# Row transposes of the rotation taken from the pair sums through DRAM, with the pair sums' additions moved behind their transposes

## The chip, the cores and the metric

One core of a Trainium2 chip runs the whole program in float32. The metric is the device time of one execution in microseconds (us). Ratios are computed as the mean time of one kernel's fast runs over the mean of the other's fast runs of the same rounds, so a ratio is not quite the quotient of the medians that stand beside it.

The engines: PE is the matrix engine, DVE the vector engine, ACT the scalar engine, Pool is GpSimd, and SP is SyncE, which here only issues DMAs. "SPq" in a profile is the queue of SP's instructions.

## The reference, cut to what matters

x is 8 images of 256 channels and 96 x 96 pixels. Two residual layers follow each other, each behind a group norm:

```python
x = x + fft_attention(gn(x))       # q, k, v = fft2(1x1 convolutions); per-head 32x32 attention of
                                   # normalized spectra; |ifft2|; 1x1 convolution
x = x + linear_attention(gn(x))    # q, k = softplus(convolutions to 32 channels)
```

The kernel never makes a spectrum. It uses that the attention needs covariances of x with itself and with x mirrored in both directions. With e = x + mirrored x and o = x - mirrored x, these are the sums of e e^T and o o^T over pixels: the **pair sums**. The value path is a multiplication of every image row by a matrix of circulant windows, called R below: the **rotation**.

## The kernel before

A batch (an image) goes through these stages: attention matrices, rotation, images (the |ifft2| and its projection), linear attention, output. The pair sums of the next batch are woven into the last three as filler for PE; what is left of them behind the output is called the tail. Batch 0's sums have nothing to be woven into and stand alone at the start.

In the pair sums, DVE or Pool add whole image rows first; PE then transposes e and o, ACT evacuates them (copies them out of PSUM, where PE has written them: 598 ns for 128x512, the median), and PE multiplies:

```python
def even_odd(b, u):                      # rows PR*u.. and their mirror (cut)
    for c in range(2):
        op = (eng.tensor_add, eng.tensor_sub)[c]
        op(d[:, :, lo:hi, 1:W], x_t[:, :, ra:ra + n, 1:W], x_t[:, :, back, W - 1:0:-1])
        ...
# pair_sums, per chunk of 128 columns:
        for c in range(2):
            for k in range(KC):
                nc.tensor.transpose(pt[...], eo[:, c, k, i:i + np_], ident)
        nc.scalar.activation(t[0:np_, :, 0:C], pt[...], AF.Copy, scale=weight)
        if pending is not None:
            products(*pending, first, False)      # acc += t^T t for e and o
```

The rotation, two rows at a time, transposes the rows again (xr), lets ACT evacuate them, and multiplies two steps later (y):

```python
nc.tensor.transpose(pt[0:W, ...], x_of(b)[:, k, o:o + W], ident)                      # xr
nc.tensor.matmul(pu[:, o:o + W + 1], lhsT=gt[0:W, r, ...], rhs=tm[:, g % TR + r, :])  # y
```

`tm` is a window of R, read from DRAM by ACT's queue in runs of 384 bytes.

## Time and profile before

| | before |
|---|---|
| time, median of 3 runs | 2765.28 us (2764.82 to 2765.53) |
| span of the profiled run | 2760.7 us |
| start to the end of batch 0's sums | 75.7 us |
| a batch (1 to 6): rotation / images / linear attention / output and what is between / tail | 73.0 / 142.0 / 69.0 / 41.1 / 14.2 to 15.3 us |

The stage times are differences between the first starts of PE's instructions that open each stage: the group norm's matmul, the images' first matmul, the second group norm, the denominators, the first output product.

The slices (each digit is a fortieth of the span, in tenths; 9 is 90% or more):

```profile
PE   8999999999999999999999999999999999999988
PEclk9999999999999999999999999999999999999997
```

PE is busy in every slice (8 or 9 tenths), and its granted clock is at 9 (90% or more) in every slice but the last, which has 7. The waits of PE (line, what it waited for, us in total, times, longest):

```profile
PE eoT L350 <- POOL eo L318: 10.4, 15, 7.3
PE kT L770 <- DVE arena L748: 3.6, 1, 3.6
PE acc L331 <- ACT xT L353: 3.5, 7, 0.5
```

All waits of PE together, 2760.7 - 2719.5 = 41 us, are smaller than 2% of the span. The table of stretches for batch 0's sums (stretch, length, busy PE, weight loads, DVE, ACT, Pool, clock, DMA share, GB/s):

```profile
0.00:20.00 20.00, 12.51 (x71) 11.29 (x72) 13.98 (x41) 5.43 (x9) 16.00 (x77) 1.00 0.94 320
20.00:60.00 40.00, 40.00 (x278) 37.50 (x277) 35.61 (x76) 13.46 (x23) 20.48 (x27) 1.00 0.37 112
60.00:75.70 15.70, 15.70 (x110) 14.75 (x109) 0.00 (x0) 5.36 (x10) 0.00 (x0) 1.00 0.16 51
```

From 20 us on PE has no gap. In the first 20 us the loads of x fill the DMA engines (share 0.94).

### The profile page before, as it was taken

How to read it: one execution, taken by the hardware profiler on the slowest of the kernel's cores; microseconds unless marked ns; L12 is line 12 of the kernel's file. 1: busy time of each engine (PE TensorE's matmuls, PEld its weight loads, DVE VectorE, ACT ScalarE, POOL GpSimd, SP SyncE). 2: the span in 40 equal slices, each digit the busy share in tenths (PEclk: the TensorE clock that was granted, in tenths of full speed). 3: DMA queues.
4: the chain of work that ended last, by engine and by line, in shares of the span. 5: the costliest groups of instructions: out<-in, count | busy, mean ns of one | idle time of the engine just before them, and what ended most of it. 6: DMA issues, size and time to landing. Idle time of an engine off the chain costs nothing.

```text
span 2760.7 us, 47785 instructions
## 1 busy us (share of the span) xinstructions
PE 2719.5 (99%) x18348; PEld 1972.5 (71%) x18348; DVE 1958.4 (71%) x4104; ACT 1366.5 (49%) x2098; POOL 841.5 (30%) x939
## 2 busy tenths in 40 slices
PE   8999999999999999999999999999999999999988
PEld 8965679657795677956679566885678856788556
DVE  7588666876668767587675875769766687676776
ACT  3455634556345563355634546345453455544553
POOL 5033340342403423035230351313513135131311
PEclk9999999999999999999999999999999999999997
DMA  5120151201512015120151201521015210251003
GB/s 169 40 65 11 47 184 43 67 9 49 179 43 73 6 47 182 43 69 6 54 179 46 63 6 54 182 54 52 7 53 184 58 46 7 62 178 28 0 7 138
DMA packets 197274, 192.50 MB, mean 70 GB/s; under 512 B 88821, under 2 KB 197049, under 8 KB 197049
## 3 DMA queue, kind: packets, MB, share of 16 engines
q1 hardware_dynamic: 129800, 164.34, 18.8%
q10 hardware_dynamic: 67248, 25.12, 3.6%
q8 instruction: 146, 2.39, 0.4%
q14 instruction: 80, 0.65, 0.1%
HBM read 113.85 MB, written 75.57 MB: 69 GB/s over the span
## 4 chain that ended last, share of the span: by engine, by line
PE 94%; DVE 3%; ACT 2%; DMA 1%; issue 1%; POOL 0%; SPq 0%; POOLq 0%; DVEq 0%; ACTq 0%
PE z L621 21%; PE po L633 18%; PE acc L331 13%; PE y L553 10%; PE xr L550 6%; PE eoT L350 5%; PE xT L779 5%; PE kq L718 5%; PE o L863 4%; PE kx L755 3%; DMA arena<-in_x_dram 1%; PE cw L423 1%; PE kT L770 1%; DVE arena L559 1%; PE mz L511 1%
## 5 line engine op out<-in xcount | busy, mean ns | idle before, releaser
L621 PE MATMUL z<-arena,mz 128*128 128x384 f32 (+2 forms) x2400 | 595.0, 476 | 0.0
L633 PE MATMUL po<-e,wo 128*128 128x384 f32 x1536 | 529.7, 486 | 0.2 <-ACT e L668 0.2
L667 POOL TENSOR_TENSOR e<-e 128x768 f32<-128x768 f32 x192 | 348.2, 1815 | 554.1 <-ACT e L666 554.1
L621 PEld LDWEIGHTS z<-arena,mz 128*128 128x128 f32 (+1 forms) x2400 | 325.6, 163 | 241.4 <-issue 42.4
L553 PE MATMUL y<-tm,xT 96*128 96x97 f32 x3040 | 472.6, 261 | 1.7 <-ACT sd_a L288 0.5
L553 PEld LDWEIGHTS y<-tm,xT 96*128 96x128 f32 x3040 | 457.8, 192 | 12.5 <-issue 4.9
L331 PE MATMUL acc<-xT 128*128 128x256 f32 (+2 forms) x2368 | 440.5, 328 | 3.5 <-ACT xT L353 3.5
L633 PEld LDWEIGHTS po<-e,wo 128*128 128x128 f32 x1536 | 289.4, 190 | 197.7 <-DVE arena L635 1.2
L662 DVE TENSOR_TENSOR e<-z,xT 128x768 f32<-128x768 f32 x384 | 365.7, 953 | 85.2 <-PE z L621 85.2
L264 DVE BATCH_NORM_STATS2 st<-arena 128x6 f32<-128x384 f32 x768 | 406.5, 552 | 13.7 <-DMA arena<-in_x_dram 3.2
L550 PE MATMUL xr<-ident,arena 128*96 128x128 f32 x1520 | 409.2, 275 | 0.0
L331 PEld LDWEIGHTS acc<-xT 128*128 128x128 f32 (+1 forms) x2368 | 380.2, 191 | 37.7 <-ACT xT L353 5.2
L563 ACT COPY xT<-xr 96x512 f32<-96x512 f32 (+1 forms) x384 | 220.2, 578 | 293.8 <-PE xr L550 289.4
L666 ACT ACTIVATE e<-e 128x1536 f32<-128x1536 f32 x192 | 284.6, 1482 | 93.5 <-DVE e L662 92.3
L668 ACT ACTIVATE e<-e 128x768 f32<-128x768 f32 x192 | 161.9, 843 | 334.0 <-POOL e L667 332.9
L317 POOL TENSOR_TENSOR eo<-arena 128x760 f32<-128x760 f32 x136 | 246.1, 1809 | 253.7 <-issue 130.1
L635 DVE TENSOR_TENSOR arena<-arena,po 128x384 f32<-128x384 f32 x384 | 211.1, 551 | 92.6 <-PE po L633 69.5
L353 ACT ACTIVATE xT<-eoT 128x512 f32<-128x512 f32 x280 | 166.6, 598 | 183.9 <-PE eoT L350 182.2
L550 PEld LDWEIGHTS xr<-ident,arena 128*96 128x96 f32 x1520 | 227.2, 150 | 10.3 <-issue 6.9
L559 DVE COPY arena<-y 128x384 f32<-128x384 f32 (+1 forms) x384 | 209.7, 547 | 1.2 <-issue 0.5
L558 DVE COPY ys<-y 128x4 f32<-128x4 f32 (+1 forms) x384 | 62.4, 162 | 199.3 <-PE y L553 195.9
L350 PE MATMUL eoT<-ident,eo 128*128 128x128 f32 (+1 forms) x1184 | 188.1, 280 | 10.4 <-POOL eo L318 10.4
(202 smaller groups left out, 2907.0 us busy)
## 6 DMA issues: line engine op xcount, KB each, us to landing
arena<-in_x_dram SPq DMA_DIRECT2D x184, 384.0 KB
out_dram<-arena SPq DMA_DIRECT2D x184, 384.0 KB
tm<-rt ACTq DMA_DIRECT2D x112, 216.0 KB
tm<-rt SPq DMA_DIRECT2D x16, 216.0 KB
arena<-in_x_dram SPq DMA_DIRECT2D x8, 288.0 KB
out_dram<-arena SPq DMA_DIRECT2D x8, 288.0 KB
wl<-in_w1t_dram SPq DMA_DIRECT2D x8, 256.0 KB
wl<-in_w2t_dram SPq DMA_DIRECT2D x8, 256.0 KB
```

Of the source, the lines that this page charges most:

```text
L264: nc.vector.bn_stats(out=st[:, k, c, :], in_=x_of(b)[:, k, c * CH:(c + 1) * CH])
L317: op(d[:, :, lo:hi, 1:W], x_t[:, :, ra:ra + n, 1:W], x_t[:, :, back, W - 1:0:-1])
L331: mm = nc.tensor.matmul(acc[c][:, m * C:m * C + (KC - m) * P], lhsT=t[0:np_, c, m * P:(m + 1) * P], rhs=t[0:np_, c, m * P:C], start=(first ...
L350: nc.tensor.transpose(pt[0:np_, c * C + k * P:c * C + (k + 1) * P], eo[:, c, k, i:i + np_], ident)
L550: nc.tensor.transpose(pt[0:W, r * C + k * P:r * C + (k + 1) * P], x_of(b)[:, k, o:o + W], ident)
L553: nc.tensor.matmul(pu[:, o:o + W + 1], lhsT=gt[0:W, r, k * P:(k + 1) * P], rhs=tm[:, g % TR + r, :], start=True, stop=True)
L559: nc.vector.tensor_copy(y[:, :, :, g + r:g + 2], src[:, :, W - 1::-1, r:2])
L621: mm = nc.tensor.matmul(out[:, o:o + n * W], lhsT=columns(mz, k, c, j), rhs=y[:, k, h * W:(h + n) * W], start=(k == 0 and o == 0), stop=(k ...
L633: nc.tensor.matmul(po[:, 0:CH], lhsT=wo[:, k, m * P:(m + 1) * P], rhs=e[:, k, :], start=(k == 0), stop=(k == KC - 1))
L662: nc.vector.tensor_add(e[:, 2 * c:2 * c + 2, :].rearrange("p t (q h) -> p t q h", h=H), pz[:, 0:CH].rearrange("p (q h) -> p q h", h=H).uns ...
L666: nc.scalar.activation(e, e, AF.Square)
L667: nc.gpsimd.tensor_add(e[:, 0:2, :], e[:, 0:2, :], e[:, 2:4, :])
```

## The change

The intent: PE transposes x itself in the pair sums, not e and o; the additions come behind the evacuation, on Pool. The transposes of six tiles of twelve are then at hand as plain transposed rows. SP writes them to DRAM (`xtd`), and the rotation reads them from there, so that PE need not transpose these rows a second time; such rows are called **spilled**. R is written once to DRAM in pieces laid out as they are used (`rx`). The diff, cut to its core:

```diff
+T0 = 6
-    for t in range(NT - 1, -1, -1):
+    for t in range(NT - 1, NT - 5, -1):
         load_x(0, t)                          # the rest is loaded tile by tile within batch 0's sums
+    rx = dram.tile([H // TR, W, TR, W + 1], F32, name="rx")
+    xtd = dram.tile([2, (H // 2 - PR * T0) * W, C], F32, name="xtd")
 ... pair_sums, per chunk j (0 to 2) of tile t:
+            if not b and j == 0 and t >= 4:
+                load_x(0, t - 4)
+            for k in range(KC):
+                nc.tensor.transpose(pt[:, 0, k * P:(k + 1) * P], front[:, k], ident)
+                nc.tensor.transpose(pt[:, 1, k * P:(k + 1) * P], back[:, i % 2, k], ident)
+            nc.scalar.activation(both, pt, AF.Copy, scale=pw[:, j:j + 1])
+            if t >= T0:
+                n = P - j // 2
+                for c in range(2):
+                    nc.sync.dma_start(out=turned(c, PR * t, 1 + P * j)[0:n], in_=both[0:n, c])
+            eo = sum_slot()[:, :, 0:C]
+            if b or j % 2:
+                nc.gpsimd.tensor_add(eo[:, 0], both[:, 0], both[:, 1])
+                nc.gpsimd.tensor_sub(eo[:, 1], both[:, 0], both[:, 1])
+            else:                             # batch 0, even chunks: DVE, straight from PSUM
+                ...
 ... rotation:
+        def spilled(h):
+            return PR * T0 <= h < H - PR * T0 and h != H // 2
+        def fetch(i):                         # three steps ahead
+            nc.sync.dma_start(out=xts[i][0:W, :, 0:C], in_=rows.rearrange("(r w) n -> w r n", w=W))
+            step(None if spilled(h) else h, ...)   # no transposes where the rows come from DRAM
```

Cut: the tables, the copies that bring the mirrored side into order (`back`; by Pool, and by ACT for tiles 0 to 5 of batches 1 to 7), the order of the pieces of R, and small changes in how often chunks are woven in.

A tile has 384 columns in three chunks of 128, shifted by one column, so that the last chunk holds one column that is not wanted. The line `n = P - j // 2` therefore leaves it out.

More of the change, by code (lines that the diff above doesn't have):

```diff
@@ L165, in two_layer_kernel, with sum_slot @@
     nc.vector.memset(xT[:, :, :, C:C + 2], 1.0)
-    turn = [0, 0]
-    def xt_slot(sums=False):
-        turn[sums] += 1
-        return xT[:, NX - 2 + turn[1] % 2 if sums else turn[0] % (NX - 2)]
+    turn = [0]
+    def sum_slot():
+        turn[0] += 1
+        return xT[:, NX - 2 + turn[0] % 2]
     at = const.tile([P, KC, NZ + 3, NH], F32, name="at")
@@ L179, in two_layer_kernel @@
     nc.scalar.dma_start(out=gri, in_=gmat)
-    half = const.tile([P, 1], F32, name="half")
-    nc.vector.memset(half, 1.0)
-    nc.vector.memset(half[0:W], 0.5 ** 0.5)
+    pw = const.tile([P, 4], F32, name="pw")
+    nc.vector.memset(pw[:, 3:4], 0.0)
+    for j in range(4):
+        nc.vector.memset(pw[32 * j:32 * j + (16, 16, 17, 1)[j], 3:4], 1.0)
+        if j != 2:
+            nc.vector.memset(pw[32 * j:32 * j + 1, 3:4], 0.5 ** 0.5)
+    nc.vector.scalar_tensor_tensor(pw[:, 3:4], in0=ident[:, 80:81], scalar=0.5 ** 0.5 - 1.0, in1=pw[:, 3:4],
+                                   op0=ALU.mult, op1=ALU.add)
+    for j in range(3):
+        nc.vector.tensor_scalar(pw[:, j:j + 1], ident[:, 95 - 32 * j:96 - 32 * j], scalar1=-1.0, scalar2=1.0,
+                                op0=ALU.mult, op1=ALU.add)
+    nc.vector.tensor_sub(pw[:, 2:3], pw[:, 2:3], ident[:, P - 1:P])
     hw2 = const.tile([P, 1], F32, name="hw2")
@@ L229, in two_layer_kernel @@
     rt = dram.tile([H, 2 * W], F32, name="rt")
+    rb = dram.tile([H, 2 * W], F32, name="rb")
+    rx = dram.tile([H // TR, W, TR, W + 1], F32, name="rx")
+    xtd = dram.tile([2, (H // 2 - PR * T0) * W, C], F32, name="xtd")
     def tables():
@@ L253, in tables, with window, turned @@
             nc.vector.tensor_copy(t0[:, o + 1:o + W], r0[:, W - 1:0:-1])
+            nc.sync.dma_start(out=rb[:, i * W:(i + 1) * W], in_=r0)
         nc.sync.dma_start(out=rt, in_=t0[:, 3 * W:5 * W])
         load_small()
-    def window(h):
-        v = rt[h:h + TR, 1:1 + W]
-        return bass.AP(v.tensor, v.offset, [[1, W], [2 * W, TR], [1, W]])
+    def window(h, n, back):
+        v = (rb if back else rt)[h:h + n, 0 if back else 1:]
+        return bass.AP(v.tensor, v.offset, [[1, W], [2 * W, n], [1, W]])
+    def turned(c, h, w):
+        return xtd[c, (h - PR * T0) * W + w:]
     def stats_chunk(st, b, c):
@@ L294, in image @@
         return t.rearrange("p k (h w) -> p k h w", w=W)
-    def even_odd(b, u):
-        assert (b, u % NT) in loaded
-        nr = PR if u < NT else 1
-        t = ring_tile(f"eo_{b}_{u}").rearrange("p (c k n) -> p c k n", c=2, k=KC)
-        x_t = image(x_of(b))
-        rows = [PR * u + i for i in range(nr)]
-        if u in (0, NT):
-            parts = [(0, 1)] + ([(1, nr)] if nr > 1 else [])
-        else:
-            parts = [(0, nr)]
-        for lo, hi in parts:
-            n = hi - lo
-            ra = x_col(rows[lo]) // W
-            rp = x_col((H - rows[lo]) % H) // W
-            back = slice(rp, rp - n if rp >= n else None, -1)
-            for c in range(2):
-                eng = nc.vector if u in (0, 1, NT) or (u == NT // 2 - 1 if b else u % 2) else nc.gpsimd
-                op = (eng.tensor_add, eng.tensor_sub)[c]
-                pop = (nc.gpsimd.tensor_add, nc.gpsimd.tensor_sub)[c]
-                d = t[:, c, :, 0:nr * W].rearrange("p k (h w) -> p k h w", w=W)
-                op(d[:, :, lo:hi, 1:W], x_t[:, :, ra:ra + n, 1:W], x_t[:, :, back, W - 1:0:-1])
-                pop(d[:, :, lo:hi, 0:1], x_t[:, :, ra:ra + n, 0:1], x_t[:, :, back, 0:1])
-        return t, nr * W
     s0 = {}
@@ L335, in products @@
                         tc.keep_in_program_order(mm)
-        pending, first = None, True
-        us = [*range(NT - 1, -1, -1), NT]
-        ahead = [even_odd(b, us.pop(0))]
-        for u in range(NT - 1, -2, -1):
-            u %= NT + 1
-            eo, cols = ahead.pop(0)
-            for i in range(0, cols, P):
-                while i == 0 and us and len(ahead) < (2 if b and u in (NT - 3, NT - 4) else 1):
-                    ahead.append(even_odd(b, us.pop(0)))
-                np_ = min(P, cols - i)
-                pt = ps_tile(f"eoT_{b}_{u}_{i}")
-                for c in range(2):
-                    for k in range(KC):
-                        nc.tensor.transpose(pt[0:np_, c * C + k * P:c * C + (k + 1) * P], eo[:, c, k, i:i + np_], ident)
-                t = xt_slot(True)
-                weight = half[0:np_] if u in (0, NT) and i == 0 else 1.0
-                nc.scalar.activation(t[0:np_, :, 0:C], pt[0:np_, :].rearrange("p (c n) -> p c n", c=2), AF.Copy,
-                                     scale=weight)
-                if pending is not None:
-                    products(*pending, first, False)
-                    first = False
-                pending = (t, np_)
-                if u < NT and i:
-                    stats_chunk(st0, b, 2 * (NT - 1 - u) + i // P - 1)
-                yield
@@ new lines, in pair_sums, with sides @@
+        x = x_of(b)
+        w0 = one.tile([P, KC, H + 1], F32, tag="ys", name=f"w0_{b}")
+        nc.gpsimd.memset(w0[:, :, H // 2:H // 2 + 1 + PR * T0], 0.0)
+        def sides(t, j):
+            o = (NT - 1 - t) * TW + (t == 0) * W + 1 + P * j
+            e = (NT - t) * TW - (t == 0) * W - 1 - P * j
+            if t or j < 2:
+                return [(0, P, x[:, :, o:o + P], x[:, :, e:e - P:-1])]
+            m = H // 2
+            rows = [x[:, :, x_col(h):x_col(h) + W] for h in (0, H // 2)] + [w0]
+            if j == 2:
+                return [(0, 32, x[:, :, o:o + 32], x[:, :, e:e - 32:-1])] + [
+                    (32 * i + 32, 32, v[:, :, 1:33], v[:, :, W - 1:W - 33:-1] if i < 2 else w0[:, :, m + 2:m + 34])
+                    for i, v in enumerate(rows)]
+            return [(32 * i, 32, v[:, :, m:m + 32], v[:, :, m:m - 32:-1]) for i, v in enumerate(rows[0:2])] + [
+                (64, 32, w0[:, :, 32:64], None), (64, 16, None, w0[:, :, m + 33:m + 49]), (80, 16, None, w0[:, :, m:m + 16]),
+                (96, 32, rows[0][:, :, 0:32], rows[0][:, :, 0:32])]
@@ new lines, in pair_sums, with turn_back @@
+        back = three.tile([P, TR * (W + 1)], F32, tag="tm", name=f"back_{b}")[:, 0:2 * C].rearrange(
+            "p (i k n) -> p i k n", i=2, k=KC)
+        def turn_back(i):
+            t, j = steps[i]
+            assert (b, t) in loaded
+            if j == 0:
+                col = x[:, :, (NT - 1 - t) * TW:(NT - t) * TW:W]
+                h, o = PR * t, H // 2 + 1 + PR * t
+                nc.gpsimd.tensor_copy(w0[:, :, h:h + PR], col[:, :, 0:PR])
+                if t:
+                    nc.gpsimd.tensor_copy(w0[:, :, o:o + PR], col[:, :, :PR - 1:-1])
+                else:
+                    nc.gpsimd.tensor_copy(w0[:, :, o:o + 1], col[:, :, 0:1])
+                    nc.gpsimd.tensor_copy(w0[:, :, o + 1:o + PR], col[:, :, 2 * PR - 2:PR - 1:-1])
+                    nc.gpsimd.tensor_copy(w0[:, :, o - 1:o], col[:, :, 2 * PR - 1:])
+            if j in (0, 3):
+                xts.append(ring_tile(f"xt_{b}_{t}_{j}").rearrange("p (j c n) -> p j c n", j=3, c=2))
+            ab = sides(t, j)
+            ready = len(ab) == 1
+            front = ab[0][2] if ready else xts[-1][:, j % 3, 0].rearrange("p (k n) -> p k n", k=KC)
+            for p0, n, *v in ab:
+                for c in range(ready, 2):
+                    if v[c] is not None:
+                        (nc.scalar.copy if b and t < T0 else nc.gpsimd.tensor_copy)(
+                            (front, back[:, i % 2])[c][:, :, p0:p0 + n], v[c])
+            return front, xts[-1][:, j % 3]
@@ new lines, in pair_sums @@
+        steps = [(t, j) for t in range(NT - 1, -1, -1) for j in range(3)] + [(0, 3)]
+        pending, first = None, True
+        xts = []
+        ahead = turn_back(0)
+        for i, (t, j) in enumerate(steps):
+            front, both = ahead
+            if not b and j == 0 and t >= 4:
+                load_x(0, t - 4)
+            if i + 1 < len(steps):
+                ahead = turn_back(i + 1)
+            pt = ps_tile(f"eoT_{b}_{t}_{j}").rearrange("p (c n) -> p c n", c=2)
+            for k in range(KC):
[4 more added lines that the diff above has]
+                n = P - j // 2
+                for c in range(2):
+                    nc.sync.dma_start(out=turned(c, PR * t, 1 + P * j)[0:n], in_=both[0:n, c])
[3 more added lines that the diff above has]
+                nc.gpsimd.tensor_sub(eo[:, 1], both[:, 0], both[:, 1])
+            else:
+                for c, op in enumerate((ALU.add, ALU.subtract)):
+                    nc.vector.scalar_tensor_tensor(eo[:, c], in0=pt[:, 0], scalar=pw[:, j:j + 1], in1=both[:, 1],
+                                                   op0=ALU.mult, op1=op)
+            if pending is not None:
+                products(*pending, first, False)
+                first = False
+            pending = (eo, P)
+            if j in (1, 2):
+                stats_chunk(st0, b, 2 * (NT - 1 - t) + j - 1)
+            if (t, j) == (T0, 2):
+                n = H // 2 - PR * T0
+                pt = ps_tile(f"w0T_{b}")
+                col = xts[-2][:, 0, 0]
+                for k in range(KC):
+                    nc.tensor.transpose(pt[0:H + 1 - PR * T0, k * P:(k + 1) * P], w0[:, k, PR * T0:H + 1], ident)
+                nc.scalar.copy(col[0:H + 1 - PR * T0], pt[0:H + 1 - PR * T0, 0:C])
+                for c in range(2):
+                    o = c * (H // 2 + 1)
+                    nc.sync.dma_start(out=xtd[c].rearrange("(h w) n -> h w n", w=W)[:, 0], in_=col[o:o + n])
+            yield
@@ L466, in attention @@
         nc.vector.scalar_tensor_tensor(rq, in0=rq, scalar=0.5 * HW, in1=tcol, op0=ALU.mult, op1=ALU.mult)
-        yield 3
+        yield 4
         for m in range(KC):
@@ L485, in attention @@
                 nc.vector.tensor_scalar_mul(sbd[s, s], l[s, :], ssum[s, :])
-            yield (5, 3)[m]
+            yield (8, 4)[m]
             pa = ps_tile(f"at_{b}_{m}")
@@ L531, in rotate, with step @@
         nc.gpsimd.memset(ys[:, :, 0:1], 0.0)
+        def spilled(h):
+            return PR * T0 <= h < H - PR * T0 and h != H // 2
         def load_r(h):
             tm = three.tile([P, TR * (W + 1)], F32, tag="tm", name=f"tm_{b}_{h}")[0:W].rearrange("p (r w) -> p r w", r=TR)
-            (nc.scalar if b else nc.sync).dma_start(out=tm[:, :, 0:W], in_=window(h))
+            if b:
+                nc.sync.dma_start(out=tm, in_=rx[h // TR])
+                return tm
+            lo = 0
+            while lo < TR:
+                back = h + lo > H // 2 and spilled(h + lo)
+                hi = lo + 2
+                while hi < TR and back == (h + hi > H // 2 and spilled(h + hi)):
+                    hi += 2
+                nc.sync.dma_start(out=tm[:, lo:hi, 0:W], in_=window(h + lo, hi - lo, back))
+                lo = hi
             nc.gpsimd.tensor_copy(tm[:, :, W:W + 1], csn[0:W, 2, h:h + TR].unsqueeze(2))
+            nc.sync.dma_start(out=rx[h // TR], in_=tm)
             return tm
-        def step(h, turned):
+        pieces = [TR * i for i in (15, 4, 0, 5, 14, 6, 1, 8, 13, 7, 2, 9, 12, 10, 3, 11)]
+        order = [h + r for h in pieces for r in range(0, TR, 2)]
+        xts = {}
+        def fetch(i):
+            if i < len(order) and spilled(order[i]):
+                xts[i] = xT[:, i % NX]
+                h = order[i]
+                c = h > H // 2
+                rows = turned(c, H - h - 1 if c else h, 0)[0:2 * W]
+                nc.sync.dma_start(out=xts[i][0:W, :, 0:C], in_=rows.rearrange("(r w) n -> w r n", w=W))
+        def step(h, due, xt=None):
             if h is not None:
                 pt = ps_tile(f"xr_{b}_{h}")
-            if turned is not None:
-                g, gt, tm = turned
+            if due is not None:
+                g, gt, tm = due
+                back = g > H // 2 and spilled(g)
                 pu = ps_tile(f"y_{b}_{g}")
@@ L550, in step @@
                         nc.tensor.transpose(pt[0:W, r * C + k * P:r * C + (k + 1) * P], x_of(b)[:, k, o:o + W], ident)
-                    if turned is not None and g + r:
+                    if due is not None and g + r:
                         o = (r * KC + k) * (W + 1)
-                        nc.tensor.matmul(pu[:, o:o + W + 1], lhsT=gt[0:W, r, k * P:(k + 1) * P], rhs=tm[:, g % TR + r, :],
+                        nc.tensor.matmul(pu[:, o:o + W + 1], lhsT=gt[0:W, 1 - r if back else r, k * P:(k + 1) * P], rhs=tm[:, g % TR + r, :],
                                          start=True, stop=True)
-            if turned is not None:
+            if due is not None:
                 src = pu[:, 0:2 * KC * (W + 1)].rearrange("p (r k w) -> p k w r", r=2, k=KC)
@@ L558, in step @@
                 nc.vector.tensor_copy(ys[:, :, g + r:g + 2], src[:, :, W, r:2])
-                nc.vector.tensor_copy(y[:, :, :, g + r:g + 2], src[:, :, W - 1::-1, r:2])
+                nc.vector.tensor_copy(y[:, :, :, g + r:g + 2], src[:, :, 0:W, r:2] if back else src[:, :, W - 1::-1, r:2])
             if h is not None:
-                xt = xt_slot()
                 r = 0 if h else 1
                 nc.scalar.copy(xt[0:W, r:2, 0:C], pt[0:W, r * C:2 * C].rearrange("p (r n) -> p r n", n=C))
-                return xt
-        tms = [load_r(g) for g in range(0, 3 * TR, TR)]
+        tms = [load_r(g) for g in pieces[0:3]]
+        pieces = pieces[3:]
         pending = []
-        for h in range(0, H, 2):
-            if h % TR == 0:
+        for i, h in enumerate(order):
+            if i % (TR // 2) == 0:
                 tm = tms.pop(0)
-            if h % TR == 4 and 3 * TR <= h - 4 + 2 * TR < H:
-                tms.append(load_r(h - 4 + 2 * TR))
-            xt = step(h, pending.pop(0) if len(pending) == 2 else None)
-            pending.append((h, xt, tm))
+            if i % (TR // 2) == 2 and i > 2 and pieces:
+                tms.append(load_r(pieces.pop(0)))
+            if not spilled(h):
+                xts[i] = xT[:, i % NX]
+            step(None if spilled(h) else h, pending.pop(0) if len(pending) == 2 else None, xts[i])
+            pending.append((h, xts.pop(i), tm))
+            fetch(i + 3)
             yield
@@ L578, in rotate @@
         y0[b] = ys
-    st1s = {}
+    st1s, kxt = {}, {}
     def images(b):
@@ L609, in images @@
         nc.vector.tensor_mul(sg[2], sg[2], sg[2])
+        kxt[b] = [three.tile([P, TR * (W + 1)], F32, tag="tm", name=f"xt{i}_{b}")[:, 0:2 * (C + 2)].rearrange(
+            "p (j n) -> p j n", j=2) for i in range(2)]
+        for t in kxt[b]:
+            nc.gpsimd.memset(t[:, :, C:C + 2], 1.0)
         st1 = new_stats(f"st1_{b}")
@@ L756, in add_kx @@
                                  rhs=xt[j // 2][:, j % 2, 0:C + 1], start=(i == 0), stop=(i == NS * CH // P - 1))
-        extra = [three.tile([P, TR * (W + 1)], F32, tag="tm", name=f"xt{i}_{b}")[:, 0:2 * (C + 2)].rearrange(
-            "p (j n) -> p j n", j=2) for i in range(2)]
-        for t in extra:
-            nc.gpsimd.memset(t[:, :, C:C + 2], 1.0)
-        slots = [*(xT[:, i] for i in range(4)), *extra]
+        slots = [*(xT[:, i] for i in range(4)), *kxt.pop(b)]
         pend = []
```

## The prediction

> **What bounds the kernel now.** I read the page's engine totals first, then the chain that ended last, then the groups, then the order of time inside one batch of the eight (each lasts about 345 us).
>
> ```profile
> span 2760.7 us, 47785 instructions
> PE 2719.5 (99%) x18348; PEld 1972.5 (71%) x18348; DVE 1958.4 (71%) x4104; ACT 1366.5 (49%) x2098; POOL 841.5 (30%) x939
> PE 94%; DVE 3%; ACT 2%; DMA 1%; issue 1%; POOL 0%; SPq 0%; POOLq 0%; DVEq 0%; ACTq 0%
> ```
>
> PE is 99% busy and is 94% of the chain, so whatever leaves PE's stream leaves the span, unless another engine makes PE wait for what remains. PE's whole idle time is 41 us, so there are hardly any waits to remove. The groups that the change touches:
>
> ```profile
> L553 PE MATMUL y<-tm,xT 96*128 96x97 f32 x3040 | 472.6, 261 | 1.7 <-ACT sd_a L288 0.5
> L550 PE MATMUL xr<-ident,arena 128*96 128x128 f32 x1520 | 409.2, 275 | 0.0
> L317 POOL TENSOR_TENSOR eo<-arena 128x760 f32<-128x760 f32 x136 | 246.1, 1809 | 253.7 <-issue 130.1 <-PE eoT L350 117.1 <-POOL eo L318 5.6
> L559 DVE COPY arena<-y 128x384 f32<-128x384 f32 x376 | 205.8, 548 | 0.0
> ```
>
> The rotation transposes each image row (xr) and multiplies it by a window of R (y). The 409 us beside xr are not what it costs: matmuls overlap[...]. The spacing of starts is the cost, and the timeline of PE in the third batch's rotation shows it:
>
> ```profile
> 815.06 0.36 PE L553 MATMUL y<-tm,xT 96*128 96x97 f32 x2
> 815.26 0.27 PE L550 MATMUL xr<-ident,arena 128*96 128x128 f32 x1
> 815.37 0.36 PE L553 MATMUL y<-tm,xT 96*128 96x97 f32 x2
> ...
> 826.06 0.27 PE L550 MATMUL xr<-ident,arena 128*96 128x128 f32 x1
> 826.17 2.15 PE L553 MATMUL y<-tm,xT 96*128 96x97 f32 x18
> ```
>
> One transpose with one y product (two passes in f32) takes 815.37 - 815.06 = 0.31 us, so a pair of rows (four of each) takes 1.23 us. At the end of the rotation 18 y passes stand alone: 2.15 us less the last one's own 0.27 is 17 spacings of 0.110 us, so eight passes alone take 0.88 us. **Removing the four transposes of a pair therefore saves 1.23 - 0.88 = 0.35 us, not four times 0.11**: a y pass behind a transpose starts sooner than a y pass behind another y pass.
>
> [...]110 ns per y pass (128 columns), and 310 - 2 x 110 = 90 ns for the transpose (96 columns). So the change is worth some 85 to 90 ns per removed transpose. [...]here 128x768 takes 1815 ns and 128x384 takes 1004 ns, hence 2.11 ns per element[...].[...]
>
> **The change, part by part.** *PE.* A tile is 4 rows and its mirror. Six tiles of twelve are spilled, rows 24 to 71 but for row 48's pair: 23 row pairs of 48. The order of the built kernel has 784 xr transposes instead of 1520, so 736 fewer, 184 pairs x 0.35 = 63 us. Added: 16 transposes for column 0 and a last chunk of 128 columns in place of 96 (32 transposes), about 2 us. The sums keep four transposes and four products per chunk. Ideal: 2765 - 61 = **2704 us**.
>
> *Sums, DVE and Pool.* Out go the additions on images (136 Pool operations of 1.81 us, 246 us; 88 on DVE, 67 us). In come 544 Pool additions of 128x256: from the two Pool durations above, 1.00 - 128 x 0.00211 = 0.73 us each, 397 us; 161 Pool copies of 128x256 at an estimated 0.6 us (128x192 takes 0.52 us here), 97 us; and some 190 small ones at about 0.25 us. Pool rises from 842 to some 1150 us, 42% of the span: no bound on average. But the additions now lie **behind** the transposes, so PE -> ACT -> Pool -> PE is a chain per chunk where it was PE -> ACT -> PE: ACT 0.69 us (the form with a column as its scale takes 686 ns here), Pool 0.73 us until the first half, some 0.1 us per hand-over.
>
> *ACT* loses 184 copies of 0.58 us (107 us) and gains 119 of 128x256 and about 120 pieces. From 843 ns at 768 and 1482 ns at 1536 elements, ACT costs 0.21 us + 0.83 ns per element: 0.42 and about 0.25 us, 80 us together.
>
> *DMA.* Per batch, 18 x 2 writes of 128 KB, 23 reads of 192 KB and 16 pieces of R of 218 KB in long runs in place of 216 KB in 384-byte ones. In the rotation the DMA share is 0.17 now (41 GB/s); 4.5 + 3.5 MB in 64 us is 125 GB/s, and the stores alone ran at 240 GB/s just before. Reads are asked for three steps ahead and used two later, some 5 us: hidden, I think.
>
> **Where part of it comes back.** Read stage by stage:
>
> ```profile
> 706.00:741.30 35.30, 35.30 (x253) 24.87 (x245) 28.38 (x57) 12.44 (x23) 20.33 (x21) 1.00 0.68 240
> 741.30:754.90 13.60, 13.60 (x97) 12.76 (x94) 9.12 (x19) 4.84 (x8) 3.91 (x8) 1.00 0.75 251
> 754.90:827.00 72.10, 71.80 (x651) 67.61 (x650) 43.79 (x149) 33.02 (x62) 2.95 (x17) 1.00 0.17 41
> ```
>
> (Columns: stretch, length, busy PE, weight loads, DVE, ACT, Pool, clock, DMA share, GB/s. They are the output stage, the tail of the next batch's sums, the rotation.)
>
> 1. *Output stage.* A chunk recurs every 2.75 us. Pool then needs 1.00 + 2 x 0.73 + about 0.2 = 2.66 us. It just fits; I charge 0.2 us per batch.
> 2. *Tail.* Seven chunks at 1.75 us with nothing else on PE. Pool needs 1.46 of 1.75, and ACT makes 17 small pieces for the last tile (4.3 us) in order with the four evacuations that PE waits for. The last tile's loads land near 744.4 to 745.1, as DVE's wait for them shows, 3 to 4 us into the tail, while ACT and Pool copies of it now stand in order ahead of chunks that are due. Following the order by hand I get 2 to 3.5 us of PE waiting: 3 per batch.
> 3. *Start of the rotation.* The attention's small matmuls wait for DVE and ACT (a table load of 1.28 us and a root lie ahead of the first of them), and row pairs fill the wait. Two of these steps are now 0.35 us shorter: about 0.7 us, plus 0.3 further on. DVE is some 85% busy in the first 15 us.
> 4. *Consecutive chunks in the linear attention* already made PE wait 0.5 us for ACT; the Pool link adds about 0.8. The end of the images: 0.2.
>
> That is 5.2 us for each of seven batches, 36 us, against 7.8 us gained in each. Batch 0 has additions on DVE, behind its tables (6 us from 26.3 to 32.9): 3 us; and windows of R read, completed and written again one after the other on SyncE, and Pool pieces in the tail: 3 us. Sum: 2765 - 61 + 36 + 6 = **2746 us**. My tail figures lean to the dark side, as waits partly overlap, so I say **2742**.
>
> **Rivals.** *All of it arrives* (2700 to 2710): for it speaks that no engine but PE is over 71% busy, and that a wait in a filler stage can be absorbed; against it, that the tail has no filler. *Pool becomes the bound of output and tail* (2775 to 2800): 2.66 of 2.75 us is close, and if the additions take 0.85 us rather than 0.73, each chunk of the output stage loses about 0.2 us, 13 chunks x 7 = 18 us, and the tail 5 us more per batch. *SyncE's order or the reads' latency starves the rotation* (2760 to 2800): a read that lands after 5 us stops PE in each of 8 spilled pieces; against it, the idle DMA in that stage. *The rotation becomes DVE's*: its two copies per pair take 0.71 us by group (0.548 + 0.164), under PE's 0.88, so not by itself.
>
> **Range and chances.** Faster by over 2% means under 2710 us, which leaves only 6 us for all waits: 0.08. Slower by over 2% means over 2820: 0.02. The rest, 0.90. Range 2712 to 2774.
>
> **What would show it.** xr x784 and y spaced 0.11 us in spilled steps (step 1); PE busy near 2655 us with idle time up from 41 to 80 or 90 us; PE's waits to be found at acc for Pool in the tail, and there for ACT; qkm waiting for DVE; no wait of y for the DMA. I am wrong if PE idles at y for reads, if the additions take other than about 0.73 us, or if the tail keeps 13.6 us.

## The result, and the profile after

The changed kernel took 2837.01 us (median of 4 runs, 2833.18 to 2844.45) beside 2765.05 us (2763.12 to 2765.53) of the kernel before: ratio 1.0265, interval 1.0241 to 1.0289. It is slower by 2.7%, and far outside the predicted range. The page's totals and slices after:

```profile
span 2832.3 us, 47838 instructions
PE 2689.0 (95%) x17628; PEld 1933.1 (68%) x17628; DVE 1932.5 (68%) x4075; ACT 1339.2 (47%) x2160; POOL 1000.7 (35%) x1405
PE   6699999999999999999999999999999999999988
PEclk8899999999999999999999999999999999999997
```

PE has 720 instructions fewer, as predicted. But it now idles 2832.3 - 2689.0 = 143 us against 41, and the first two slices (142 us) have fallen to 6 tenths, with a lower granted clock (the clock that PE is allowed at that moment, as a share of its full one). The groups:

```profile
L329 PE MATMUL acc<-xT 128*128 128x256 f32 (+1 forms) x2368 | 459.1, 336 | 41.2 <-POOL xT L408 41.1
L652 PE MATMUL y<-tm,xT 96*128 96x97 f32 x3040 | 416.2, 269 | 4.9 <-ACT xT L661 4.2
L408 POOL TENSOR_TENSOR xT<-xt 128x256 f32<-128x256 f32 x272 | 204.1, 751 | 116.5 <-ACT xt L401 111.7
L649 PE MATMUL xr<-ident,arena 128*96 128x128 f32 x784 | 204.6, 276 | 0.0
```

xr is down to 784, y waits almost only for ACT (4.2 of its 4.9 us) and not for the reads from DRAM, and an addition on Pool takes 751 ns. The rotation does what it should. The waits of PE:

```profile
PE acc L329 <- POOL xT L408: 41.1, 49, 4.0
PE eoT L399 <- DMA arena<-in_x_dram: 30.2, 5, 10.5
PE eoT L400 <- POOL back L383: 21.3, 6, 6.6
PE xT L882 <- DVE xT L887: 10.5, 14, 1.2
PE qkm L461 <- issue: 7.7, 7, 1.1
```

The waits for loads of x and for Pool's copy `back`, which stands behind the same loads, come to 51 us, and all eleven lie in the first 138 us. (qkm is a small matmul of the attention at the start of the rotation; its new wait of 1.1 us per batch will matter at the end of the experiments.) The stages (in us, from the starts on PE):

| stage | before | after | difference |
|---|---|---|---|
| batch 0's sums | 75.7 | 137.8 | +62.1 |
| rotation, per batch | 73.0 | 66.0 | -7.0 |
| images | 142.0 | 141.8 | -0.2 |
| linear attention | 69.0 | 72.6 | +3.6 |
| to the first output product | 8.3 | 9.4 | +1.1 |
| output | 32.8 | 32.6 | -0.2 |
| tail | 14.2 to 15.3 | 18.7 to 21.6 | +4.8 (means) |
| batch 7 from its attention to its last output product | 298.1 | 293.5 | -4.6 |

The middle rows nearly cancel: from the end of batch 0's sums to the start of batch 7's attention the kernel before took 2378.9 us and the changed one 2392.5. So the whole is 62.1 + 13.6 - 4.6 = 71.1 us, and the spans differ by 71.6. **Most of the loss, 62 of 71 us, is in the first 138 us.** PE has about the same work there as before (458 matmul records against 454), but it is idle for 52.1 us instead of 7.5, and busy for 85.7 us instead of 68.2. Most of the second difference goes with the clock: each of PE's six waits of 4.5 to 10.5 us behind its first matmul in this stretch was followed, 2.3 to 5.4 us after it began, by 6.8 or 10.2 us at a granted clock of 0.50. 25.8 us of PE's busy time fell into these stretches; if it was slowed in proportion, that is an estimated 13 us. So of the 62 us some 45 are waits, and of the other 17 most, by this estimate, is work at the lower clock behind them. What happens there is seen in the stretches of the changed kernel:

```profile
20.00:60.00 40.00, 22.40 (x112) 19.42 (x110) 13.49 (x48) 7.31 (x12) 8.67 (x22) 0.73 0.35 117
37.00:40.00 3.00, 0.00 (x0) 0.00 (x0) 0.00 (x0) 0.00 (x0) 0.00 (x0) 0.75 1.05 378
60.00:100.00 40.00, 27.42 (x154) 23.66 (x153) 16.40 (x36) 7.37 (x11) 9.96 (x22) 0.84 0.18 52
118.00:120.00 2.00, 0.00 (x0) 0.00 (x0) 0.00 (x0) 0.00 (x0) 0.00 (x0) 0.50 0.07 25
```

Look at the last two columns. For some microseconds the DMA engines are full (share 1.05, 378 GB/s); in others they move 24 or 25 GB/s with a share of 0.07, and 0.07 x 16 is 1.1, as much as one engine of sixteen. In both of the short stretches shown every engine of the core stands still. In between PE works on what has landed, with the DMA still moving 24 GB/s at a share of 0.07 (45 to 49 us: PE 4.00 of 4.00 us busy). The DMA's average of 0.35 hides two quite different states. SP's queue in order of time (start, duration, line, operation, how many):

```profile
15.91 5.96 SPq L139 DMA_DIRECT2D arena<-in_x_dram  x2
21.96 8.07 SPq L405 DMA_DIRECT2D xtd<-xt  x6
30.08 5.98 SPq L139 DMA_DIRECT2D arena<-in_x_dram  x2
36.16 8.07 SPq L405 DMA_DIRECT2D xtd<-xt  x6
```

Six writes (a tile) hold the issuing queue for 8 us and two loads for 6, so a tile takes 14 us, and loads of x that PE needs stand behind them. (The issue of one load took up to 5.3 us; the median of all 200 is 0.38.)

The views don't say which transfers move at 24 GB/s. What sets two of a tile's six writes apart is their row count: 127 rows of 1 KB, where the others have 128. My estimate goes by it: if it is these two, they take 2 x 127 x 1024 B / 24 GB/s = 10.8 us per tile, and six such tiles 65 us. The measured difference is 62; that the two are near is no proof, since the 62 are made of waits and of a lower clock. Whether this is the cause, the experiments must say.

### The profile page after: what moved, and what is told of

The parts are those of the page before. It is cut to its first block, busy times and chain, and to the rows that moved or that the text cites.

```text
span 2832.3 us, 47838 instructions
## 1 busy us (share of the span) xinstructions
PE 2689.0 (95%) x17628; PEld 1933.1 (68%) x17628; DVE 1932.5 (68%) x4075; ACT 1339.2 (47%) x2160; POOL 1000.7 (35%) x1405
## 5 line engine op out<-in xcount | busy, mean ns | idle before, releaser
L329 PE MATMUL acc<-xT 128*128 128x256 f32 (+1 forms) x2368 | 459.1, 336 | 41.2 <-POOL xT L408 41.1
L329 PEld LDWEIGHTS acc<-xT 128*128 128x128 f32 x2368 | 390.2, 194 | 89.1 <-POOL xT L408 52.2
L652 PE MATMUL y<-tm,xT 96*128 96x97 f32 x3040 | 416.2, 269 | 4.9 <-ACT xT L661 4.2
L652 PEld LDWEIGHTS y<-tm,xT 96*128 96x128 f32 x3040 | 406.2, 192 | 15.8 <-issue 7.3
L401 ACT ACTIVATE xt<-eoT,pw 128x512 f32<-128x512 f32 x296 | 202.4, 686 | 201.6 <-PE eoT L400 188.2
L742 DVE TENSOR_TENSOR arena<-arena,po 128x384 f32<-128x384 f32 x384 | 211.4, 552 | 92.5 <-PE po L740 68.2
L408 POOL TENSOR_TENSOR xT<-xt 128x256 f32<-128x256 f32 x272 | 204.1, 751 | 116.5 <-ACT xt L401 111.7
L661 ACT COPY xT<-xr 96x512 f32<-96x512 f32 (+1 forms) x200 | 113.8, 573 | 274.1 <-PE xr L649 272.3
L409 POOL TENSOR_TENSOR xT<-xt 128x256 f32<-128x256 f32 x272 | 205.4, 755 | 0.0
L649 PE MATMUL xr<-ident,arena 128*96 128x128 f32 x784 | 204.6, 276 | 0.0
L971 DVE TENSOR_TENSOR arena<-arena,o 128x384 f32<-128x384 f32 x288 | 142.6, 550 | 54.0 <-PE o L966 53.9
L399 PE MATMUL eoT<-ident,arena 128*128 128x128 f32 x560 | 150.0, 294 | 30.2 <-DMA arena<-in_x_dram 30.2
```

The source lines that it names most:

```text
L329: mm = nc.tensor.matmul(acc[c][:, m * C:m * C + (KC - m) * P], lhsT=t[0:np_, c, m * P:(m + 1) * P], rhs=t[0:np_, c, m * P:C], start=(first ...
L409: nc.gpsimd.tensor_sub(eo[:, 1], both[:, 0], both[:, 1])
L649: nc.tensor.transpose(pt[0:W, r * C + k * P:r * C + (k + 1) * P], x_of(b)[:, k, o:o + W], ident)
L652: nc.tensor.matmul(pu[:, o:o + W + 1], lhsT=gt[0:W, 1 - r if back else r, k * P:(k + 1) * P], rhs=tm[:, g % TR + r, :], start=True, stop=True)
L742: nc.vector.tensor_add(x[:, m, n], x[:, m, n], po[:, 0:CH])
```

## The experiments

All are edits of the changed kernel, and all results were correct but for f3, which is wrong on purpose. The first four ran with three rounds each beside a kernel before at 2765.45 us, the next four with five rounds beside 2763.46, the last four with five rounds beside 2764.72. The three groups ran on three different chips, so kernels of different groups are better compared by their ratios to the kernel before than by their medians.

### e1_rows128: whole writes

```diff
-    xtd = dram.tile([2, (H // 2 - PR * T0) * W, C], F32, name="xtd")
+    xtd = dram.tile([2, (H // 2 - PR * T0 + 1) * W, C], F32, name="xtd")
-                n = P - j // 2
+                n = P
```

The unwanted row falls on a place that the next write fills (room is added at the end, which the write of column 0 leaves out).

> The changed kernel, but the third write of a tile takes 128 rows instead of 127 (one more row of DRAM holds the row too many, and column 0 is written over later). Theory (a transfer of 127 rows goes through one of the 16 DMA engines, 10.6 us per spilled tile, and holds up everything behind it in SyncE's queue): the first mean over x falls from 137 us back to 75 to 80 us, the whole from 2837 to 2765 to 2778. Rival (SyncE's order: loads of x stand behind writes that wait for ACT): no change, 2830 to 2845. Rival (writing 1 KB rows to DRAM is slow as such): no change either.

Measured: 2776.22 us (2772.88 to 2777.62), ratio 1.0036, interval 1.0024 to 1.0048. Batch 0's sums took 91.1 us in place of 137.8, the tail 16.5 to 17.7 in place of 18.7 to 21.6, and the other stages of batches 0 to 6 were as in the changed kernel within 0.4 us. (The rotation of batch 7 was 3 us longer; see the end of the experiments.) The total came as expected; batch 0's sums did not come down to the expected 75 to 80. The stretches and SP's queue of this run:

```profile
20.00:60.00 40.00, 36.66 (x244) 33.31 (x242) 27.27 (x76) 12.83 (x19) 16.89 (x37) 1.00 0.38 112
60.00:91.10 31.10, 28.32 (x165) 24.30 (x166) 16.02 (x35) 9.80 (x16) 16.25 (x52) 0.89 0.73 219
```

```profile
9.74 4.01 SPq L405 DMA_DIRECT2D xtd<-xt  x6
14.47 1.35 SPq L139 DMA_DIRECT2D arena<-in_x_dram  x2
17.83 4.30 SPq L405 DMA_DIRECT2D xtd<-xt  x6
```

With one row more in each of two writes per tile, the six issues take 4 us rather than 8, the loads 1.3 rather than 6, and PE's busy time between 20 and 60 us goes from 22.40 to 36.66 of 40. One row was worth 61 us in all, 47 of them in batch 0's sums.

### e2_loads_first: the loads no longer behind the writes

All loads of batch 0's x are issued at the start, as in the kernel before; the 127 rows stay.

```diff
-    for t in range(NT - 1, NT - 5, -1):
+    for t in range(NT - 1, -1, -1):
-            if not b and j == 0 and t >= 4:
-                load_x(0, t - 4)
```

> The changed kernel, but batch 0's loads of x are all issued at the start, as in the kernel before, ahead of the writes; the writes stay at 127 rows. Rival (order of SyncE's queue is the cause): batch 0's sums take 75 us again, 2765 to 2780. Theory (one engine for 127 rows): loads no longer stand behind the slow transfers, but 12 transfers of 127 KB still take 64 us on one engine and hold the four buffers that they read: only part comes back, 2785 to 2815.

Measured: 2840.08 us (2833.24 to 2844.62), ratio 1.0267. Batch 0's sums took 116.6 us, 21 less, but the rotation of batch 0 then took 80.8 instead of 65.8. In the sums ACT waited 27.6 us, in three waits, until writes had freed the buffers that it fills; then PE's y waited 11.3 us once for a window of R, which stood behind the writes. (The rotation of batch 1 took 70.8 us; it holds 10.2 us at a granted clock of 0.50, of the kind treated at the end of the experiments, and is not counted here.) So with 127 rows the order of the queue decides only who waits. The rival that blamed the order falls, and my own figure of a partial gain was wrong as well.

### e3_split112: 127 rows as 112 and 15

```diff
-                    nc.sync.dma_start(out=turned(c, PR * t, 1 + P * j)[0:n], in_=both[0:n, c])
+                    for lo, hi in ((0, P),) if n == P else ((0, 112), (112, n)):
+                        nc.sync.dma_start(out=turned(c, PR * t, 1 + P * j)[lo:hi], in_=both[lo:hi, c])
```

> The changed kernel with each write of 127 rows cut into 112 and 15 rows: the same bytes, one issue more. Theory (the count of 127 rows decides, not the bytes): as with 128 rows, within 5 us, 2765 to 2780. If the rows' content or the place in DRAM mattered, no change.

Measured: 2781.09 us (2780.19 to 2781.99), ratio 1.0055; batch 0's sums 93.2 us. The same rows and bytes as in the changed kernel, two writes more per tile, and 56 us less (the total is 1 us above the expected range; two of its rotations are 5 us longer, with the clock at 0.50 for 10.2 us each). It is the row count of a write that matters, not its bytes, its place or the odd row itself.

### e4_no_spill: the sums' new form alone

No writes; every row is transposed in the rotation, as before.

```diff
-            if t >= T0:
+            if False:
             ...
-            return PR * T0 <= h < H - PR * T0 and h != H // 2
+            return False
```

> The changed kernel without any spill: sums from transposed x with additions behind, R in pieces, but every row transposed again in the rotation and nothing written or read by way of DRAM. It leaves the cost of the sums' new form alone. Theory: batch 0 takes 75 to 80 us again; the rotation is back at 73 us; tail, linear attention and output keep their 3 to 9 us of waits per batch: 2790 to 2825. If those waits come from the DMA traffic of the spill, they vanish as well: 2765 to 2775.

Measured: 2813.20 us (2811.41 to 2814.2), ratio 1.0173. Batch 0's sums 82.0 us, rotation 72.3 to 73.1, linear attention 72.9, tail 16.5 to 17.7. The sums' new form (with R in pieces) thus costs 48 us, as expected, and with whole writes (e1) the path through DRAM gives 37 of them back. So two halves of the change work against each other, and the gain of the rotation is real.

### f1_rows_loads: e1 and e2 together

```diff
+    xtd = dram.tile([2, (H // 2 - PR * T0 + 1) * W, C], F32, name="xtd")
+                n = P
+    for t in range(NT - 1, -1, -1):           # all loads of batch 0 at the start
```

> The changed kernel with full writes of 128 rows and, in addition, all loads of batch 0's x issued at the start. The run with 128 rows alone still had 8.8 us of waits of eoT for loads of x in batch 0. If these loads stand behind the small weight loads and the writes in SyncE's queue, batch 0's sums shrink from 91.1 to about 84 us and the total from 2776 to 2766 to 2771. If the kernel of full rows was limited there by Pool's pieces, the total stays at 2774 or more.

Measured: 2769.0 us (2764.54 to 2778.1, 15 runs), ratio 1.0024, interval 1.0016 to 1.0032; batch 0's sums 82.6 us. With whole writes the early loads do help in batch 0's sums (91.1 to 82.6); in the total the intervals of e1 and f1 overlap. Against the kernel before, the profiled run of f1 adds up like this: +6.9 in batch 0's sums, about -55 in eight rotations, +28 in seven linear attentions, +8 on the way to the output, +17 in seven tails, -3 elsewhere: +2 us. The spans differ by 2.1. The profiled run is the fastest of the 15, 4.5 us below their median, so some microseconds of the typical run aren't in this sum.

### f2_tail_dve: the copies of the last tile on DVE

Edit to f1; the wait for the last tile's load would no longer hold ACT.

```diff
-                        (nc.scalar.copy if b and t < T0 else nc.gpsimd.tensor_copy)(
+                        (nc.vector.tensor_copy if b and not t else nc.scalar.copy if b and t < 6 else nc.gpsimd.tensor_copy)(
```

> As f1, and the copies of the last tile (tile 0, batches 1 to 7) are VectorE's instead of ScalarE's, so that the wait for the late load of that tile no longer holds back ScalarE's evacuations of earlier chunks. Theory (ScalarE's order holds the tail): the tail of a batch shrinks by 1.5 to 2.5 us, 10 to 17 us below f1 in all. Rival (the load itself ends last, whoever waits for it): within 4 us of f1, as VectorE then waits in the same place.

Measured: 2767.53 us (2761.53 to 2778.04, 21 runs), ratio 1.0017, interval 1.001 to 1.0024. The tails are 16.4 to 17.7 us against 16.6 to 18.0. The theory that ACT's order holds the tail falls.

### f3_pool_copies: additions replaced by copies, wrong result on purpose

```diff
-                nc.gpsimd.tensor_add(eo[:, 0], both[:, 0], both[:, 1])
-                nc.gpsimd.tensor_sub(eo[:, 1], both[:, 0], both[:, 1])
+                nc.gpsimd.tensor_copy(eo[:, 0], both[:, 0])
+                nc.gpsimd.tensor_copy(eo[:, 1], both[:, 1])
```

> Wrong result on purpose: as f1, with Pool's two-input additions of the sums (addition and subtraction, batches 1 to 7 and the odd chunks of batch 0) made one-input copies of the same size. Theory (Pool's additions with two inputs collide with VectorE's in the linear attention): the stretch from the second group norm to the denominators shrinks from 72.9 to 70 us or less, VectorE's softplus instructions there return to about their lengths of the kernel before, and the total falls 20 us or more below f1. Rival (the order of the work or the yields that were changed costs it): 72 us or more stay, and VectorE's lengths return with no effect on the total, within 6 us of f1.

Measured: 2740.82 us (2734.56 to 2750.57), ratio 0.992. The linear attention took 70.2 us in every batch (72.9 in f1), the way to the output 9.0 (9.4), the tail 15.8 to 16.4 (16.6 to 18.0). The groups of two of DVE's softplus instructions (line, operation, count, busy us, mean ns of one, idle time before), first before the change, then in f1, then here:

```profile
L747 DVE TENSOR_TENSOR arena<-arena 128x384 f32<-128x384 f32 x96 | 52.2, 550 | 0.5
L745 DVE SCALAR_TENSOR_TENSOR arena<-spu,arena 128x384 f32<-128x384 f32 x96 | 51.7, 551 | 0.6
```

```profile
L850 DVE SCALAR_TENSOR_TENSOR arena<-spu,arena 128x384 f32<-128x384 f32 x96 | 64.7, 685 | 0.5
L852 DVE TENSOR_TENSOR arena<-arena 128x384 f32<-128x384 f32 x96 | 62.5, 656 | 0.5
```

```profile
L850 DVE SCALAR_TENSOR_TENSOR arena<-spu,arena 128x384 f32<-128x384 f32 x96 | 58.7, 623 | 0.6
L852 DVE TENSOR_TENSOR arena<-arena 128x384 f32<-128x384 f32 x96 | 55.3, 582 | 0.5
```

The same DVE instruction grew from 551 to 685 ns on average when Pool's additions were placed beside it, and went halfway back when these became copies. The mean hides two cases: before the change all 96 of the SCALAR_TENSOR_TENSOR took 541 to 568 ns; in f1 the median is still 551, but 29 took over 700 and up to 1086 ns; with the copies the longest took 793. An addition has two inputs and a copy one, but Pool's copies are shorter than its additions as well (0.40 us against 0.73 where nothing disturbs them), so this run does not part the effect of the second input from that of the length. Why DVE's instructions grow beside them is not shown. What PE waited for in seven linear attentions shows two costs: before the change 3.5 us for ACT at the products and 2.0 for DVE; in f1 12.4 us for Pool's additions at the products and 17.3 for DVE's copies (xT and kx); here 8.6 for Pool, 2.3 for DVE and 3.5 for ACT.

### f4_ten_tiles: eight tiles of twelve through DRAM

Edit to f1 (the label is a misnomer: tiles 4 to 11 are eight):

```diff
-T0 = 6
+T0 = 4
-                        (nc.scalar.copy if b and t < T0 else nc.gpsimd.tensor_copy)(
+                        (nc.scalar.copy if b and t < 6 else nc.gpsimd.tensor_copy)(
```

> As f1, with the transposes of 8 tiles of 12 written to DRAM instead of 6. Theory (with whole writes DRAM costs nothing on the path, and the gain scales with the row pairs not transposed): 8 more row pairs x 0.35 us = 2.8 us per batch off the rotation, 66.0 to about 63.2, total 18 to 24 us below f1. Rival (DMA engines or SyncE's queue are the limit of the rotation or of the images): the rotation stays above 65, or waits of y for DMA appear, and the total is no more than 8 us below f1.

Measured: 2845.85 us (2841.4 to 2862.78), ratio 1.0312. The rotation fell to about 64.1 us where it was undisturbed, 1.9 and not 2.8 below f1, and the tail rose to 23.8 to 25.8. In batch 0 the sums took 94.2 us and the rotation some 8 us more than in f1, and y waited 7.2 us in all for the reads from DRAM. Most of the loss, about 53 of the 81 us between the two profiled runs, is in the seven tails. The waits of ACT in one of them have one line that says why:

```profile
ACT xt L383 <- DMA arena<-in_x_dram: 7.3, 1, 7.3
```

The writes of tiles 5 and 4 now stand in SP's queue during the output stage. In the tail of the fourth batch's sums, which begins at 1127.3 us, the loads of the last tile were issued at 1130.40 us, 3 us into it; in f1 they were issued 2 us before the same tail began. The rival holds: with more spilled tiles the order in SP's one queue makes the tail's loads late.

### g1_early_chunks: six chunks of the sums moved ahead of the softplus

Edit to f1: chunks are woven in beside the kq products instead.

```diff
-            yield 0.5
+            yield 1.25
             ...
-                yield 0.25
+                yield 0
```

> As f1, with the six chunks of the next batch's sums that lay beside the softplus instructions (24 steps of 0.25) moved ahead of them, beside the kq products (eight steps of 1.25 instead of 0.5). Theory (Pool's two-input additions slow VectorE's two-input softplus instructions when both run at once): the stretch from the second group norm to the denominators shrinks from 72.9 to 70 to 71.5 us, xT's waits for VectorE (10.5 us in all) fall below 4, and the total is 10 to 20 us below f1. Rival (the same work meets the same collision elsewhere, or Pool's 1.5 us a chunk now bounds the kq stretch): the stretch stays at 72.5 or more and the total within 5 us of f1.

Measured: 2769.48 us (2759.05 to 2775.57, 22 runs), ratio 1.0015. The linear attention stayed at 72.7 us. Its parts show what happened: the stretch with the chunks grew from 18.2 to 26.5 us, the one without them shrank from 36.9 to 28.3, and the waits of xT for DVE fell from 10.5 only to 8.4 us. Of DVE's two instructions one shortened (SCALAR_TENSOR_TENSOR, 685 to 608 ns) and the other grew (TENSOR_TENSOR, 656 to 685). So the chunks cost as much in the one place as in the other, and the expected gain was wrong: the move does not remove the collision. PE's waits in the stretch fell from 4.2 to 3.1 us per batch, but its busy time grew from 68.6 to 69.6 with the same matmuls; no run shows why.

### g2_tail_split, g3_both, g4_three

g2 (edit to f1) gives half of the last tile's additions to DVE:

```diff
-            if b or j % 2:
+            if (t or j % 2 == 0) if b else j % 2:
                 nc.gpsimd.tensor_add(eo[:, 0], both[:, 0], both[:, 1])
```

> As f1, with the additions of chunks 1 and 3 of the last tile (tile 0, batches 1 to 7) on VectorE straight from PSUM, as batch 0's even chunks have them, and those of chunks 0 and 2 still on Pool. Theory (the tail is Pool's 1.5 us a chunk and the latency of its two additions behind the last evacuation): the tail of a batch falls from 16.7 to 18.0 to about 15.5, 7 to 12 us off f1's total. Rival (the late load of tile 0 sets the tail): under 4 us.

Measured: 2769.87 us (2760.87 to 2779.04), ratio 1.0019. The tails are 16.4 to 18.0 us, no shorter than f1's beyond 0.3 us. The theory falls in this form: PE's waits for Pool in seven tails fell from 9.9 to 7.1 us, but 2.2 us of waits for DVE came in their place.

g3 is g1 and g2 together, and g4 is g3 and f2 together.

> g1 and g2 together. If both theories hold the gains add: 17 to 30 us below f1, at 2740 to 2752 us, 0.4 to 0.9% below the kernel before. If only one holds, its gain alone.

> g3 and f2 (the copies of tile 0 on VectorE instead of ScalarE) together. With the additions out of the way ScalarE's wait for the late load may be what is left of the tail: 3 to 10 us below g3. Rival (f2 showed under 2 us): within 3 us of g3, or above it since VectorE now does both.

Measured: g3 2762.95 us (2759.26 to 2769.75, 13 runs), ratio 0.9997, interval 0.9989 to 1.0005; g4 2772.4 us (2770.34 to 2783.04), ratio 1.0037. g3 is the best correct version found, and it equals the kernel before; the expected 2740 to 2752 us did not come. By the ratios it is some 7 us below f1, and its profile shows no stage shorter than in g1 or g2 by more than some tenths. g4 is worse: DVE then has the copies and the additions of the last tile, and its tails are 17.8 us in every batch.

The runs of these last kernels scatter by 10 to 18 us (g4's by 13), those of the kernel before by 8. The stretches of g2 show from where. Its third and second batch, each from the start of the rotation:

```profile
770.00:780.00 10.00, 10.00 (x46) 7.70 (x45) 6.06 (x17) 1.53 (x3) 0.00 (x0) 0.72 0.29 82
```

```profile
431.00:441.00 10.00, 10.00 (x68) 8.38 (x67) 6.01 (x17) 2.00 (x4) 0.00 (x0) 1.00 0.34 87
```

The granted clock was 0.72 in one and 1.00 in the other (the column after Pool's), and the rotations took 70.9 and 66.0 us. Such rotations, 3 to 5 us longer, occur in none to three batches of a profiled run of the last eight kernels (f4 has other long ones too). Differences under some 5 us between these kernels should therefore not be explained.

The traces do show where these events begin. In every kernel that spills, PE waits 1.10 us for qkm near the start of the rotation of batches 1 to 7; the kernel before and e4, which don't spill, have no such wait and no such event. In the seven last kernels without f4 there are 49 of these waits, and behind nine of them, 0.8 to 1.4 us after the wait began, the granted clock fell to 0.50 for 6.8 or 10.2 us. Each rotation that was 3 to 5 us longer holds one of the nine. Why behind these nine and not behind the other 40 is not shown, and no run closed the wait (by weaving more row pairs into it, say). So it is a reading of the traces and not a tested cause; if it holds, much of the scatter is a cost of the spill.

## Why the prediction was wrong, by its steps

**What bounds the kernel; the saving in PE.** Right. 736 transposes less made the rotation 7.0 us shorter per batch (predicted 7.8 less 1.0 at its start; the wait for qkm there is 1.1 us). What the prediction did not see is that this wait is at times followed by a granted clock of 0.50. That a transpose saves only its spacing and not its duration was the right reading: by durations the 736 would have been worth 736 x 0.275 = 202 us. The reason given for the 0.35 us, that a y pass behind a transpose starts sooner than one behind a y pass, is not what the starts show: the pass behind a transpose comes after 113 ns, passes alone follow each other after 112, and the short distance, 86 ns, is that of the second y pass behind the first. The sum is right all the same. PE's busy time was forecast near 2655 us and was 2689.0, with 17 of the difference in batch 0's sums (2672.1 in f1).

**The paragraph on DMA is the step that failed.** It reckoned bytes per batch and GB/s, found the DMA idle, and ended "hidden, I think". It looked only at the reads in the rotation, and counted all 36 writes of a batch as 128 KB and alike, though twelve of them have 127 rows. In its place the trace showed stretches of 24 GB/s at a share of 0.07, as much as one engine, beside 378 GB/s at 1.05, and the runs that it is the writes of 127 rows that cost the time. **The step "batch 0: 3 + 3 us" was +62 us.** Whole writes alone took 61 us off the total, 47 of them there (e1), a split in 112 and 15 rows took 56 off (e3), and another order in the queue took nothing off (e2). With whole writes alone batch 0's sums stay at +15.4 us; with early loads as well, which the predicted kernel didn't have, at +6.9 (f1). That this is near to the 6 predicted is luck. The same writes also cost about 2 us in each tail: it was 16.5 to 17.7 us in e1 against 18.7 to 21.6.

**Rival 3 came near and named the wrong place.** It feared SP's order and its reads for the rotation. SP's queue was indeed where the time went, by its writes, in the sums of batch 0. The rotation of the changed kernel had no wait for the DMA, as the prediction said.

**Pool's additions.** 0.73 us predicted, 0.75 measured. Pool's copies were put at 0.6 us and take 0.43 on average. Pool as the bound of the output stage did not come: that stage is 0.2 us shorter, where 0.2 us was charged.

**The linear attention** was mis-sized: "about 0.8" us was the hand-over through Pool; it cost 3.6 us, and 1.1 on the way to the output. In f1 PE's waits for the sums' products there went from 0.5 us per batch to 1.8, so this term is 1.3 and not 0.8; its waits for DVE's copies went from 0.3 to 2.5, and these the prediction did not have at all. The prediction asked whether Pool had time for its additions, and not what they would do to DVE's. f3 gave 2.7 of the 3.9 us back. That Pool's additions cost this is shown; that the second input alone does is not.

**The tail**: 3 us predicted, 4.8 measured, of which some 2 belong to the 127 rows. One reason given for it (ACT's copies behind a late load) did not hold: without them on ACT nothing was won (f2), nor with half of the additions on DVE (g2). The other, that PE would wait at the products for Pool, did: in f1 all of PE's waits in seven tails, 9.9 us, are of this kind, against 1.7 us of waits in the tails before the change. Shorter Pool instructions in their place (f3) took 1.1 us off each tail. So about half of the remaining 2.4 us goes with the length of Pool's additions; the other half stays open.

**The sum.** With the row count mended, the prediction's parts would have been -61 + 36 + 6; measured in f1, which also has the early loads, they are about -55 + 50 + 7. (The 36 contain 7 us at the start of the rotations, which the -55 have already taken in.) That is +2 us rather than -19: within the two per cent, at the upper end of the range. With the row count alone mended (e1) the kernel took 2776.2 us, 2 us above the range: the linear attention and the load order of batch 0 were mis-sized as well.

## What to carry to other kernels

Look at the row count of every DMA that a change adds, not only at its bytes: here two writes of 127 rows per tile cost 61 us against 128 rows (e1), and 56 against 112 and 15 (e3), so one row more or a split can be worth more than the whole change. Where a profile shows all engines idle and a low DMA share at once, read the share in short stretches; here a share of 0.07 with a waiting queue was as much as one engine of sixteen at work (24 GB/s), not a free DMA. A wait of the matrix engine can cost more than its own length: look at the granted clock behind it (here 0.50 for 6.8 or 10.2 us behind each of six waits in batch 0's sums). And where an engine off the critical path gets more work, ask what happens to the engines beside it (here DVE's SCALAR_TENSOR_TENSOR of 128x384 went from 551 to 685 ns on average with Pool's additions beside it), since free time alone doesn't tell.
